# A graph layer on one core: 71 instead of 24 rows per step fetched one by one

## The chip, the cores and the metric

The kernel runs on one core of a Trainium2 chip. The metric is the device time of one execution in microseconds (us). A core has five engines with queues of their own: TensorE (PE; its weight loads are listed as PEld), VectorE (DVE), ScalarE (ACT), GpSimd (POOL) and SyncE (SP). SP and ACT can issue DMAs whose descriptors hardware makes; POOL's indirect DMA gathers rows by a list of numbers.

## The reference

The kernel computes one layer of message passing over a graph with 50000 nodes of 128 features and 1650000 edges, sorted by their target node:

```python
Xs = X[src]
m_data = Xs @ W_data.T + b_data
m_ctrl = Xs @ W_control.T + b_control
msg = jnp.where((edge_types == 0)[:, None], m_data, m_ctrl)
agg = jax.ops.segment_sum(msg, dst, num_segments=X.shape[0])
x = _layernorm(x + relu(agg + (X @ W_self.T + b_self)), axis=-1)
```

Each edge takes the row of its source node, multiplies it with one of two matrices, by the edge's type, and adds the result to its target node. Then come the node's own product, a relu, the residual and a normalisation of each row. Source nodes are random; the targets come in ascending order.

## The kernel before

Sums and matrices change places: the kernel first adds up the source rows of each target and type, and multiplies the sums with the two matrices afterwards. It goes over the edges in blocks (`NBLK` of them, all unrolled into one program). A block has two steps (`Q`), and a step three kinds of edges:

- 12 chunks (`R`) of 128 edges. `gathers` (L477) has POOL fetch 128 source rows of 512 bytes with one indirect DMA (L483), 24 of them a block. Six make a pass (`PASS`), with one buffer `y` a pass out of ten (`SLOTS`); the first gather of a pass waits until PE has read its buffer. In `products` (L494) PE multiplies the rows with a one-hot matrix of the targets (`oh`, which DVE makes in `onehot`, L411), and adds up into `acc` (L502).
- 43 fill edges (`F`) that `fill` (L308) puts in place of edges from a node to itself, which need no gather.
- `S` single rows, 24 of them in the kernel before. `single_rows` (L443) fetches each with a DMA of its own of 512 bytes, 12 of a step's on SP and 12 on ACT (`TURNS`). They land in one tile `yx` of `S` partitions, of which there are four (`ROW_SLOTS`), and are one more matmul a step (L508).

The byte offset of each single row is worked out by DVE (`offsets`, L432, tile `at_x`), loaded into registers by the queue that issues (a register load, L452), and moved into the DMA's address (a MOVE and the DMA, both L457). `LOADS` tells in how many portions the rows of a block are loaded and issued. A portion is at most 32 registers a queue:

```python
return min(n, 32 * part)
```

The rows of block b are asked for two blocks ahead (`AHEAD`). PE waits for all of them at once, when the first step of the block ends (`rows_fetched`, L462, a wait at L466 on one counter for each queue). PE takes its work in order, so that everything behind this wait waits too: the two products of single rows, the second step, `layer` (L533) of this block, and the sums that DVE takes from `acc` (`add`, L514).

The loop from L628 on writes the order of every engine's instructions out by hand. For block b, with its four passes numbered q:

- q = 0: six gathers and their products; `layer` and `moments` of block b-1; the one-hot matrix of b+2; portion 0 of the single rows of b+2.
- q = 1: six more, and the row product; ACT's `root` (L563) for the two blocks before, every second block; `counts` of b+2 (L422); portion 1, if there is one.
- q = 2: `columns` of the next group of ten blocks (`GB`), once a group; DVE's `store` (L572), which waits for the root; `left_out_rows`, and `fill` of b+5; portion 2, if there is one.
- q = 3: `left_out_matrix` of b+5; `offsets` of b+3 (L437); SP's `store_rows` (L577), which waits for `store`.

SP also loads a tile `xT` a block (L408), three blocks ahead, and once a group the lists of the next group (L167, L170, L172, L300, L305). Register loads of block places are at L401 (SP) and at L515 and L525 (DVE).

Of the kernel before, what the change touches and what calls it, by code (L numbers as in the profile page):

```python
# [38 lines left out]
B = 112  # L39
C = R * Q  # L40
F = 43
TURNS = (12, 12)
S = sum(TURNS)
LOADS = 1
BEGIN = (0, -(-Q * TURNS[0] // 4) * 4)
X = BEGIN[1] + -(-Q * TURNS[1] // 4) * 4
R1 = R + 1
# [36 lines left out]
def plain(b):  # L84

    return b == 0 or b >= NBLK - 1
# [6 lines left out]
def straight(ctx, tc, c, x, x_t, edges_t, edges_f, src_x, dst_first, first_p, out):  # L93
# [324 lines left out]
    def counts(b):  # L418

        cnt = ohp.tile([P, Q, 2 * W], BF16, name="cnt")  # L420
        with nc.allow_low_precision(reason="whole numbers up to R1"):
            nc.vector.tensor_reduce(cnt, ohs[b].rearrange("p (q r) w -> p q w r", r=R1), AX.X, ALU.add)  # L422
        cnts[b] = cnt
# [8 lines left out]
    def offsets(b):  # L432

        if not plain(b):
            g, i = divmod(b, GB)
            ats[b] = stp.tile([1, X], I32, name="at_x", bufs=AHEAD + 2)
            nc.vector.tensor_scalar(ats[b], one_g[g][:, i * X:(i + 1) * X], float(ROW), None, op0=ALU.mult)  # L437

    def part_of(n, part):

        return min(n, 32 * part)

    def single_rows(b, part):  # L443

        if part == 0:
            ys[b] = stp.tile([S, Q, D], F32, name="yx", bufs=ROW_SLOTS)
        both = []
        for j, (eng, dma) in enumerate(((SP, nc.sync), (ACT, nc.scalar))):
            n = Q * TURNS[j]
            k0, k1 = part_of(n, part), part_of(n, part + 1)  # L450
            at = BEGIN[j]
            _, rows = nc.values_load_multi_w_load_instructions(ats[b][0:1, at + k0:at + k1], engines=[eng], **RANGE)  # L452
            both.append([(dma, fetched[j][b % ROW_SLOTS], *divmod(k0 + k, TURNS[j]), sum(TURNS[:j]), row)
                         for k, row in enumerate(rows)])
        for pair in zip_longest(*both):
            for dma, sem, q, k, at, row in filter(None, pair):
                copy = dma.dma_start(ys[b][at + k:at + k + 1, q, :].bitcast(U8), x_bytes[:, bass.ds(row, ROW)])  # L457
                copy.then_inc(sem, 16)
                tc.no_tile_sem_insts.add(copy.ins.name)
                tc.add_to_no_dep_group(f"single{b}", copy.ins)  # L460

    def rows_fetched(b):  # L462

        times = len(range(b % ROW_SLOTS or ROW_SLOTS, b + 1, ROW_SLOTS))
        for j in range(2):
            wait = nc.tensor.wait_ge(fetched[j][b % ROW_SLOTS], 16 * Q * TURNS[j] * times)  # L466
        tc.declare_fence(wait.ins, group=f"single{b}")
# [149 lines left out]
    for b in range(1, RAHEAD):  # L617
# [3 lines left out]
        if b < AHEAD:  # L621
            onehot(b)
            counts(b)
            for part in range(LOADS):
                single_rows(b, part)
        if b == 1:
            clear_sums()
    for b in range(NBLK + 1):  # L628
# [16 lines left out]
        for q, (step, ks) in enumerate(passes_of(b)):  # L645
# [26 lines left out]
            if q == 3:  # L672
                left_out_matrix(b + RAHEAD)
                offsets(b + AHEAD + 1)
            if q < LOADS and not plain(b + AHEAD):
                single_rows(b + AHEAD, q)
# [336 lines left out]
```

## Time and profile before

| | |
|---|---|
| median of 3 runs | 18214.56 us (18202.21 to 18215.72) |
| the profiled execution | 18215.72 us, span 18214.0 us |
| blocks, gathers | 515; 12336 + 18 |
| single rows on SP and on ACT | 12312 each |
| busy: POOL, DVE, PE | 11699.9, 11018.7, 7203.9 us |
| DVE's costliest line (L422, `counts`) | 2973.1 us, 5773 ns each |
| the root on ACT (L563) | 258 times 295 ns |
| mean granted TensorE clock | 0.589 |

The profile's page gives the busy time of each engine, DMA queues (q0 has POOL's gathers, q1 what SP issues, q10 what ACT issues), and groups of instructions by line. A group's row has its count, its total and its mean duration, then the idle time of the engine before its instructions and what ended it: "issue" is time in which the profile shows no wait, "remote" an event that it can't put down to an engine. Instructions that issue DMAs on SP and ACT, moves and register loads are not counted as busy; they are seen in the timeline and in the answers for single lines.

### The profile page before, as it was taken

What the parts mean: (1) busy time and instruction counts of PE and PEld (TensorE: products, weight loads), DVE (VectorE), ACT (ScalarE), POOL (GpSimd) and SP (SyncE); (2) the same over time, 40 slices, a digit from 0 to 9 for tenths busy, and PEclk for the clock granted to TensorE, in tenths of its full rate; (3) what the DMA queues carried; (4) which work ended last, traced back from release to release, by engine and by line L of the source; (5) the groups of instructions that cost most, each with busy time, mean ns of one, the idle gap of its engine ahead of it and who ended that gap; (6) DMA issues with size and microseconds to landing.
All of it is one profiled execution on the core that took longest, in us unless ns stands there. A gap on an engine that the chain in (4) does not pass through costs nothing.

```text
span 18214.0 us, 162871 instructions
## 1 busy us (share of the span) xinstructions
PE 7203.9 (40%) x36190; PEld 6305.2 (35%) x36191; DVE 11018.7 (60%) x13887; ACT 79.5 (0%) x264; POOL 11699.9 (64%) x12364
## 2 busy tenths in 40 slices
PE   3343333433433333444333334443444334333344
PEld 3333333333333333333333333333333333333333
DVE  6666666566656656666666666666566666656555
ACT  0000000000000000000000000000000000000000
POOL 6666666666666666666666666666666666666665
PEclk6555555556555566555565555556555555656655
DMA  2222212222222221222222222222222222222221
GB/s 54 50 52 52 52 51 51 52 51 52 52 52 51 51 52 51 52 51 52 52 51 52 52 51 52 51 52 51 52 52 51 52 51 52 52 52 52 51 51 47
DMA packets 604666, 938.00 MB, mean 51 GB/s; under 512 B 308795, under 2 KB 392578, under 8 KB 603676
## 3 DMA queue, kind: packets, MB, share of 16 engines
q0 software_dynamic: 395392, 810.40, 17.6%
q1 hardware_dynamic: 183222, 110.53, 2.3%
q10 hardware_dynamic: 25062, 6.55, 0.2%
q8 instruction: 295, 4.83, 0.1%
q14 instruction: 695, 5.69, 0.1%
HBM read 896.80 MB, written 29.71 MB: 51 GB/s over the span
## 4 chain that ended last, share of the span: by engine, by line
DVE 44%; another core or an unknown queue 26%; PE 16%; issue 12%; ACTq 1%; DVEq 1%; DMA 0%; ACT 0%
DVE cnt L422 14%; PE acc L502 10%; DVE by L337 5%; DVE new L321 4%; DVE m L318 4%; DVE v_new L325 4%; DVE old L334 3%; PE po L541 2%; PE po L539 1%; ACTq L457 1%; DVE pl L369 1%; PE acc L508 1%; PE po L538 1%; DVE sums L518 1%
## 5 line engine op out<-in xcount | busy, mean ns | idle before, releaser
L483 POOL DMA_INDIRECT y<-in_x,idx x12336 | 11681.0, 947 | 6471.0 <-issue 3401.7
L502 PE MATMUL acc<-oh,y 128*128 128x120 f32 x24708 | 5141.9, 376 | 1832.3 <-issue 1828.4
L502 PEld LDWEIGHTS acc<-oh,y 128*128 128x128 f32 x24708 | 4697.9, 283 | 1955.6 <-issue 1952.4
L344 PE MATMUL small<-ones_b,by 128*86 128x1 bf16 x513 | 118.6, 231 | 7600.8 <-DVE by L337 5791.1
L422 DVE TENSOR_REDUCE cnt<-oh 128x240 bf16<-128x3120 f32 x515 | 2973.1, 5773 | 0.1
L344 PEld LDWEIGHTS <-by 128*86 128x86 bf16 x513 | 75.0, 146 | 7806.7 <-DVE by L337 5949.2
L547 DVE COPY h<-po 112x128 f32<-112x128 f32 x515 | 150.3, 292 | 4041.0 <-remote 2349.9
L414 DVE TENSOR_TENSOR oh<-col,small 128x3120 f32<-128x3120 f32 x515 | 1736.2, 3371 | 0.0
L518 DVE TENSOR_TENSOR sums<-acc,sums 128x180 f32 x1030 | 355.5, 345 | 2007.5 <-remote 1512.5
L337 DVE TENSOR_REDUCE by<-old 128x86 bf16<-128x1118 f32 x513 | 1110.8, 2165 | 19.1 <-DVE old L334 1.4
L508 PE MATMUL acc<-oh,yx 24*128 24x120 f32 x2052 | 648.3, 396 | 209.7 <-issue 209.2
L318 DVE TENSOR_TENSOR m<-rk,small 128x1118 f32<-128x1118 f32 x513 | 677.2, 1320 | 20.6 <-DVE small L316 2.8
L321 DVE TENSOR_TENSOR new<-m,small 128x1118 f32<-128x1118 f32 x513 | 677.3, 1320 | 17.6
L325 DVE TENSOR_REDUCE v_new<-new 128x26 f32<-128x1118 f32 x513 | 676.1, 1318 | 17.6
L334 DVE TENSOR_TENSOR old<-m,small 128x1118 f32<-128x1118 f32 x513 | 673.3, 1312 | 0.0
L508 PEld LDWEIGHTS acc<-oh,yx 24*128 24x128 f32 x2052 | 414.2, 244 | 391.7 <-issue 350.6
L541 PE MATMUL po<-wmsgT,sums 128*112 128x128 f32 x2060 | 526.6, 400 | 0.0
L351 DVE COPY at<-small 86x1 f32<-86x1 f32 x513 | 79.1, 154 | 614.7 <-remote 330.9
L539 PE MATMUL po<-bias,sums 3*112 3x128 f32 x1030 | 353.0, 438 | 242.1 <-issue 120.2
L511 PE MATMUL acc<-cnt,to_row 128*128 128x60 bf16 x2060 | 289.0, 211 | 362.0 <-issue 361.6
L541 PEld LDWEIGHTS po<-wmsgT,sums 128*112 128x112 f32 x2060 | 382.1, 255 | 109.9 <-issue 89.9
L539 PEld LDWEIGHTS po<-bias,sums 3*112 3x112 f32 x1030 | 207.0, 255 | 371.0 <-issue 229.8
(118 smaller groups left out, 4109.8 us busy)
## 6 DMA issues: line engine op xcount, KB each, us to landing
y<-in_x,idx POOLq DMA_INDIRECT x12336
yx<-in_x ACTq DMA_DIRECT2D x12312, 0.5 KB
yx<-in_x SPq DMA_DIRECT2D x12312, 0.5 KB
xT<-in_x_t SPq DMA_DIRECT2D x515, 56.0 KB
out<-o SPq DMA_DIRECT2D x515, 56.0 KB
vf_all<-vd SPq DMA_DIRECT2D x52, 430.0 KB
sdt<-in_edges_t SPq DMA_DIRECT2D x52, 390.0 KB
one_g<-in_src_x SPq DMA_DIRECT2D x52, 1.9 KB
```

What stands on the lines that cost most here:

```text
L318: nc.vector.tensor_tensor(m, rk_g[g][:, i, :, None].to_broadcast([P, C1, F]), rank_no_ps[:, None, :].to_broadcast([P, C1, F]), op=ALU.is_e ...
L321: nc.vector.tensor_tensor(new.rearrange("p (q r) f -> p q r f", r=R1), m.rearrange("p (q r) f -> p q r f", r=R1), vf.rearrange("p (q f) -> ...
L325: nc.vector.tensor_reduce(v, new, AX.X, ALU.add)
L334: nc.vector.tensor_tensor(old, m, cb[:, :, None].to_broadcast([P, C1, F]), op=ALU.mult)
L337: nc.vector.tensor_reduce(by, old.rearrange("p (q r) f -> p q f r", r=R1), AX.X, ALU.add)
L414: nc.vector.tensor_tensor(oh, col_g[g][:, i, :, None].to_broadcast([P, C1, 2 * W]), num_ps[:, None, :].to_broadcast([P, C1, 2 * W]), op=AL ...
L422: nc.vector.tensor_reduce(cnt, ohs[b].rearrange("p (q r) w -> p q w r", r=R1), AX.X, ALU.add)
L483: copy = nc.gpsimd.indirect_dma_start(out=y[:r, k % PASS, :].bitcast(U8), out_offset=None, in_=x_rows, in_offset=bass.IndirectOffsetOnAxis ...
L502: nc.tensor.matmul(acc[:, :2, :].rearrange("p t w -> p (t w)"), y[:r, k % PASS, :], ohs[b][:r, column(k), :], start=k == of_step[0], stop= ...
L508: nc.tensor.matmul(acc[:, :2, :].rearrange("p t w -> p (t w)"), ys[b][:, q, :], ohs[b][:S, q * R1 + R, :], start=False, stop=True)
L539: nc.tensor.matmul(po, a[0:3, 2, :B], bias, start=False, stop=False)
L541: nc.tensor.matmul(po, a[:, t, :B], c["wmsgT"][:, t * D:(t + 1) * D], start=False, stop=t == 1)
```

## The change

```diff
-TURNS = (12, 12)
+TURNS = (35, 36)
 S = sum(TURNS)
-LOADS = 1
+LOADS = 3
```

A step now has 71 single rows, 35 on SP and 36 on ACT; a block has 70 and 72. They are loaded and issued in three portions: 32, 32 and 6 on SP, 32, 32 and 8 on ACT. All else follows from these constants: a block covers 3300 edges (3206 before), so there are 501 blocks (515 before); `yx` has 71 partitions and `at_x` 144 numbers (48 before); the second and third portion of a block's rows are issued behind its second and third pass, on ACT behind the root.

## The prediction

> **What bounds the kernel now.** I read the page first: which engine fills the span.
>
> ```profile
> span 18214.0 us, 162871 instructions
> ...
> PE 7203.9 (40%) x36190; PEld 6305.2 (35%) x36191; DVE 11018.7 (60%) x13887; ACT 79.5 (0%) x264; POOL 11699.9 (64%) x12364
> ...
> q0 software_dynamic: 395392, 810.40, 17.6%
> q1 hardware_dynamic: 183222, 110.53, 2.3%
> q10 hardware_dynamic: 25062, 6.55, 0.2%
> ...
> L483 POOL DMA_INDIRECT y<-in_x,idx x12336 | 11681.0, 947 | 6471.0 <-issue 3401.7
> ...
> L508 PE MATMUL acc<-oh,yx 24*128 24x120 f32 x2052 | 648.3, 396 | 209.7 <-issue 209.2
> ```
>
> POOL's gathers, busy time plus the idle before them, are 11681 + 6471 = 18152 us: the whole span. So I looked at POOL in order of time (start, duration, idle before):
>
> ```profile
> 9257.74 0.95 POOL L483 DMA_INDIRECT y<-in_x,idx  x1 [0.31 <-issue]
> 9258.99 0.95 POOL L483 DMA_INDIRECT y<-in_x,idx  x1 [0.30 <-issue]
> 9262.92 0.95 POOL L483 DMA_INDIRECT y<-in_x,idx  x1 [2.98 <-remote]
> 9264.17 0.95 POOL L483 DMA_INDIRECT y<-in_x,idx  x1 [0.30 <-issue]
> ```
>
> A gather follows the last after 1.25 us, and about every twelfth after 3.8 us. Counted over the trace: 11304 intervals of 1.252 us and 1049 long ones, mean 3.83. A block has 24 gathers and mostly two long intervals: 24 x 1.252 + 2 x 2.58 = 35.2 us, and 513 such blocks are 18.06 ms. The buffer that a long interval waits for had been read by PE a median 10 us before, so this is mostly POOL's own pace, not PE's. DVE is busy 11018.7 / 515 = 21.4 us of a block and comes second.
>
> Then the two queues that the change loads, SP and ACT. In SP's timeline (start, length, what):
>
> ```profile
> 9171.70 21.93 SPq L457 DMA_DIRECT2D yx<-in_x  x24
> 9193.71 0.67 SPq L408 DMA_DIRECT2D xT<-in_x_t  x1
> 9204.60 20.41 SPq L457 DMA_DIRECT2D yx<-in_x  x24
> 9229.67 2.10 SPq L577 DMA_DIRECT2D out<-o  x2
> 9232.82 0.70 SPq L408 DMA_DIRECT2D xT<-in_x_t  x1
> 9241.50 22.82 SPq L457 DMA_DIRECT2D yx<-in_x  x24
> ```
>
> 24 single rows occupy SP for 20 to 23 of 35 us, although the median register move and the median issue of one are short (ns: least, median, most):
>
> ```profile
> L457 SPq MOVE yx<-in_x x12312: 2/29/1467, 33.1 to 18157.1; - x199
> L457 SPq DMA_DIRECT2D yx<-in_x x12312: 2/228/1487, 34.5 to 18157.8; - x199
> ```
>
> So I split one burst: first ten microseconds with gathers running, then three in which POOL paused.
>
> ```profile
> 9251.17 8.52 SPq L457 DMA_DIRECT2D yx<-in_x  x6
> ```
>
> ```profile
> 9261.77 2.55 SPq L457 DMA_DIRECT2D yx<-in_x  x7
> ```
>
> ```profile
> 9251.00:9261.00 10.00, 0.38 (x2) 0.10 (x1) 8.25 (x7) 0.00 (x0) 6.80 (x8) 0.63 0.20 53
> 9261.20:9264.20 3.00, 0.00 (x0) 0.00 (x0) 2.86 (x6) 0.00 (x0) 0.98 (x2) 0.50 0.00 1
> ```
>
> The last two lines are windows; the last two numbers of each are the DMA share and GB/s. With gather packets moving (0.20, 53 GB/s) a row takes SP 1.4 us; with none (0.00, 1 GB/s) 0.36 us. Over the whole trace I called a moment "traffic" when a q0 packet was in flight or had ended within 1.3 us: 88.6% of the time. In bursts SP spends 1.19 us a row in traffic and 0.43 out of it; ACT 0.84 and 0.353. SP alone, with ACT and PE idle, still needs 1.26 in traffic: the cause is not the other queue's rows. What the mechanism is I can't say.
>
> **The change, part by part.**
>
> *Fewer blocks.* A step takes 1536 + 43 + 71 = 1650 edges instead of 1603, a block 3300 instead of 3206. 1650000 - 3072 = 1646928 edges give 499 full middle blocks (513 before) and a rest of 228 in 2 gathers (2250 in 18 before). Gathers: 24 + 499 x 24 + 2 = 12002 instead of 12354. At 18177.5 / 12354 = 1.471 us each, the 352 that go are worth -518 us if POOL stays the bound: 17.70 ms. DVE and PE lose 14 blocks as well.
>
> *More rows on SP and ACT.* SP issues 2 x 35 = 70 a block instead of 24, ACT 72. This decides. SP's other work in a block: three register loads instead of one. The rows for them:
>
> ```profile
> L452 SPq TENSOR_LOAD <-at_x x513: 8/1583/1603, 31.7 to 18126.8; - x171
> ```
>
> ```profile
> L515 DVEq TENSOR_LOAD <-place_i x1030: 298/304/548, 90.9 to 18203.1; - x172
> ```
>
> 24 registers 1.583 us, one 0.304: (1.583 - 0.304) / 23 = 0.056 a register. Loads of 32, 32 and 6 are 2.04 + 2.04 + 0.58 = 4.7 us (before 1.6). With 1.2 us of stores (2.1 to 2.6 per two blocks), about 0.5 for xT and 1.1 for moves, waits on semaphores and a tenth of a group's lists, 7.5 us.
>
> Traffic lasts 0.886 x 35.37 = 31.3 us a block, set by 24 gathers and as long afterwards. If SP's 7.5 us fall outside it, SP issues 31.3 / 1.19 = 26.3 rows in traffic and the other 43.7 in 18.8 us: 31.3 + 18.8 + 7.5 = 57.6 us. If they all fall inside, 23.8 / 1.19 = 20 rows and then 50 x 0.43 = 21.5: 52.8 us. I take the middle, 55.2, against 35.2 of POOL. ACT: 31.3 / 0.84 = 37.3 rows, 34.7 x 0.353 = 12.2, loads 5.0: 48.5, under SP. The price from both sides: 70 x 0.43 + 7.5 = 37.6 us if all rows went at the quiet rate, 70 x 1.19 + 7.5 = 90.8 if none did. I stay between because POOL must pause once it is ten passes ahead of PE, and PE waits at L466 for the rows: the pauses are where SP catches up.
>
> Two pages of the Trainium skill say something else here. "DMA: Bandwidth & Descriptors", section "Issuing engines are not separate DMA queues", has the sequencer's time to start a DMA as usually small relative to the DMA; here ACT's q10 moved 25062 packets in 0.2% of 16 engines' span, some 23 ns each, beside 840 ns of issue, so the trace says the reverse for these rows, and by the rule the sum would be 17.70 ms. "Runtime: NRT & Kernel Launch", section "Instruction fetch mechanics", gives about 200 ns a register for such loads; an estimate from it is 14 us a block and some 32 ms, and the row of 1.583 us for 24 decides against it.
>
> *Who waits.* PE stops at L466 in mid-block; behind it stand the last row products, two passes, and DVE's sums. On ACT the root of a pair now stands behind 32 rows instead of 24 and ahead of 40; DVE's stores, `fill` and `offsets` stand behind it. With PE waiting for rows DVE has 55 - 21 us to spare, so I cost it at nothing; if that cover were gone it is up to (2.1 + 32 x 0.84) / 2 = 14.5 us a block. SP's stores come 46 rows later, with `o` in 4 buffers, and xT is asked for three blocks ahead: nothing. POOL's order is the same.
>
> *Small parts.* L508 contracts 71 rows instead of 24: the rows with 3 (438 ns, L539) and 128 partitions (400 ns, L541) differ little, 0. `at_x` grows from 1x48 (185 ns) to 1x144; 1x520 takes 412 ns (L201), so at most 0.1 us a block on a DVE that waits, 0 here. A group's row list is 5.6 KB instead of 1.9, one DMA in ten blocks: 0.
>
> *Sum.* 499 x 55.2 = 27545 us; ahead of SP's first row are 34 us and behind its last 56: **27.6 ms**, made against a span of 18214.0 us (execution 18215.7, median of the runs 18214.6).
>
> **Rivals.**
> 1. *The queues keep up, POOL stays the bound: 17.70 ms, faster.* It needs a block of SP under 36.2 us (18214 less 90, over 501), so a row in (36.2 - 7.5) / 70 = 0.41 us on average. For it: the medians (29 and 228 ns) and the quiet stretch (0.36). Against: 88.6% of the time is traffic.
> 2. *The queues almost keep up:* the slow spells fade once POOL waits, all rows go at 0.43: 37.6 us, 18.9 ms. Against: traffic can't be less than 24 gathers of 1.25 us a block.
> 3. *SP goes at ACT's rates* (0.84, 0.353): 46.0 to 50.3 us, 23.0 to 25.2 ms. For it: nothing in the rows tells why SP is the slower.
> 4. *Traffic spreads over the longer block*, so today's mean of 0.91 us in the bursts holds (21.9 / 24): 70 x 0.91 + 7.5 = 71.2 us, 35.6 ms. For it: PE frees buffers a pass at a time.
>
> **How the numbers follow.** Forecast 0.65 (23 to 33 ms with its own doubts), rival 1 0.07, 2 0.04, 3 0.12, 4 0.12. The range takes in rival 3 and reaches towards 4: 23.0 to 34.0 ms. About 0.2% is what a measurement tells from no change; cases 2, 3, 4 and the forecast are slower, rival 1 faster, and 0.01 lies between: 0.07, 0.01, 0.92.
>
> **What would show it.** Right: the rows' issues fill SP from end to end, 70 in 45 to 50 us; POOL's idle time doubles or more and its releaser is PE; PE's idle moves to L508 or the fence before it; block period near 55 us. Wrong: SP idle at 0.4 us a row (rival 1 or 2); ACT full and SP waiting; or DVE's `rstd` waiting for `sd` at length, which would make ACT's order, not SP's rate, the cause.

## The result and the profile after

The changed kernel takes 25257.88 us (median of 4 runs, 25222.15 to 25267.41) against 18208.39 us: 1.3871 times as long, 95% interval 1.3847 to 1.3895. It is slower, as forecast, and inside the range (23.0 to 34.0 ms), 8.5% under the 27.6 ms named.

For what follows one thing must be known: the experiments ran on four chips of two kinds. On chips 1 and 2 the kernel before takes 18.24 and 18.05 ms, as above; on chips 3 and 4 it takes 15.47 ms. Every ratio below is to the kernel before on the same chip. I call them 18 ms chips and 15 ms chips; the measurement above belongs with the first. Each chip was used in one session, so that the kind may be a chip's own or a condition it was in.

The page of the changed kernel (first run, profiled; span 25253.8 us): the lines that answer to those of before, and the shares of the chain that ended last.

```profile
span 25253.8 us, 254178 instructions
...
PE 6887.4 (27%) x35177; PEld 6389.4 (25%) x35178; DVE 10793.1 (43%) x13519; ACT 77.3 (0%) x257; POOL 11344.9 (45%) x12012
...
SPq 60%; issue 35%; DMA 2%; PE 1%; DVE 1%; ACTq 0%; another core or an unknown queue 0%; PEldq 0%; ACT 0%; DVEq 0%
SPq L457 51%; SPq L452 8%; DMA yx<-in_x 1%; DMA out<-o 1%; SPq L408 1%; PE acc L508 1%; SPq L401 0%; DVE cnt L422 0%; PE acc L502 0%; SPq L577 0%; ACTq L457 0%; DVE by L337 0%; PE pl L363 0%; DVE sums L518 0%
...
L483 POOL DMA_INDIRECT y<-in_x,idx x12000 | 11341.5, 945 | 13814.1 <-PE acc L502 9126.1
...
L508 PE MATMUL acc<-oh,yx 71*128 71x120 f32 x1996 | 595.2, 392 | 12940.7 <-PEq L466 12755.7
```

POOL, DVE, ACT and PE's products are busy for less time than before (PE's weight loads 1% longer), and the span is 7 ms longer. The chain now runs through SP: L457 (row moves and issues) 51%, L452 (row loads) 8%, and 35% "issue", time in which the queue waited for nothing that is shown. POOL's idle time has doubled, 13.8 ms against 6.5, and is ended mostly by PE's reading of buffers (L502, 9.1 ms). PE in turn stands 12.8 ms in front of L508, released by the fence of L466.

SP's timeline of two blocks (start, length, what):

```profile
12004.63 47.44 SPq L457 DMA_DIRECT2D yx<-in_x  x70
12052.16 0.36 SPq L408 DMA_DIRECT2D xT<-in_x_t  x1
12054.78 45.40 SPq L457 DMA_DIRECT2D yx<-in_x  x70
12100.35 2.03 SPq L577 DMA_DIRECT2D out<-o  x2
```

70 rows fill 45 to 47 us, loads included, and SP goes from one block's rows to the next block's without a wait. POOL in the same stretch:

```profile
12035.20 0.94 POOL L483 DMA_INDIRECT y<-in_x,idx  x1 [0.30 <-issue]
12036.45 0.94 POOL L483 DMA_INDIRECT y<-in_x,idx  x1 [0.30 <-issue]
12057.59 0.94 POOL L483 DMA_INDIRECT y<-in_x,idx  x1 [20.20 <-PE acc L502]
```

POOL gathers for some 31 us and then stands for 20. The windows just before and inside this stand (the last two numbers are the DMA share and GB/s), and SP's rows in each:

```profile
12020.00:12036.00 16.00, 5.64 (x24) 4.86 (x23) 4.35 (x5) 0.00 (x0) 10.24 (x11) 0.50 0.19 47
12039.50:12057.00 17.50, 3.64 (x19) 3.53 (x20) 2.73 (x2) 0.00 (x0) 0.00 (x0) 0.50 0.03 6
```

```profile
12018.84 17.57 SPq L457 DMA_DIRECT2D yx<-in_x  x18
```

```profile
12039.21 12.86 SPq L457 DMA_DIRECT2D yx<-in_x  x35
```

18 rows in 17.6 us with gathers running, 35 in 12.9 us without, with one register load among them each time. That is the loss in one view: POOL must stand still before SP can catch up.

### The profile page after: what moved, and what is told of

Same layout as the page of the kernel before. It is cut to its first block, busy times and chain, and to the rows that moved or that the text cites. A ratio compares the mean times of both kernels' runs of the same rounds, so it can differ in the third digit from the quotient of the medians.

```text
span 25253.8 us, 254178 instructions
## 1 busy us (share of the span) xinstructions
PE 6887.4 (27%) x35177; PEld 6389.4 (25%) x35178; DVE 10793.1 (43%) x13519; ACT 77.3 (0%) x257; POOL 11344.9 (45%) x12012
## 4 chain that ended last, share of the span: by engine, by line
SPq 60%; issue 35%; DMA 2%; PE 1%; DVE 1%; ACTq 0%; another core or an unknown queue 0%; PEldq 0%; ACT 0%; DVEq 0%
SPq L457 51%; SPq L452 8%; DMA yx<-in_x 1%; DMA out<-o 1%; SPq L408 1%; PE acc L508 1%; SPq L401 0%; DVE cnt L422 0%; PE acc L502 0%; SPq L577 0%; ACTq L457 0%; DVE by L337 0%; PE pl L363 0%; DVE sums L518 0%
## 5 line engine op out<-in xcount | busy, mean ns | idle before, releaser
L483 POOL DMA_INDIRECT y<-in_x,idx x12000 | 11341.5, 945 | 13814.1 <-PE acc L502 9126.1
L502 PE MATMUL acc<-oh,y 128*128 128x120 f32 x24004 | 5037.4, 396 | 9.3 <-issue 9.2
L502 PEld LDWEIGHTS acc<-oh,y 128*128 128x128 f32 x24004 | 4800.3, 305 | 10.5 <-issue 10.3
L508 PE MATMUL acc<-oh,yx 71*128 71x120 f32 x1996 | 595.2, 392 | 12940.7 <-PEq L466 12755.7
L508 PEld LDWEIGHTS acc<-oh,yx 71*128 71x128 f32 x1996 | 421.3, 263 | 13061.4 <-PEq L466 12872.7
L538 PE MATMUL po<-wselfT,xT 128*112 128x128 f32 x1002 | 310.0, 412 | 0.0
L531 DVE TENSOR_TENSOR sums<-pl,sums 128x336 f32<-128x336 f32 x499 | 253.4, 508 | 79.1 <-issue 63.0
L511 PEld LDWEIGHTS <-to_row 128*128 128x128 bf16 x2002 | 264.4, 132 | 32.6 <-issue 4.5
```

Of the source, the lines that this page charges most:

```text
L483: copy = nc.gpsimd.indirect_dma_start(out=y[:r, k % PASS, :].bitcast(U8), out_offset=None, in_=x_rows, in_offset=bass.IndirectOffsetOnAxis ...
L502: nc.tensor.matmul(acc[:, :2, :].rearrange("p t w -> p (t w)"), y[:r, k % PASS, :], ohs[b][:r, column(k), :], start=k == of_step[0], stop= ...
L508: nc.tensor.matmul(acc[:, :2, :].rearrange("p t w -> p (t w)"), ys[b][:, q, :], ohs[b][:S, q * R1 + R, :], start=False, stop=True)
```

## The experiments

| kernel (single rows a step on SP, ACT) | chip | us | against before there |
|---|---|---|---|
| changed (35, 36) | as above, 18 ms | 25258 | 1.387 [1.385, 1.390] |
| changed, again | 1, 18 ms | 25337 | 1.389 [1.387, 1.391] |
| changed, again | 2, 18 ms | 24923 | 1.381 (one run) |
| changed, one gather a pass | 1, 18 ms | 15460 | 0.848 (one run) |
| changed, one gather a pass | 3, 15 ms | 15413 | 0.996 (one run) |
| changed, three gathers a pass | 3, 15 ms | 15581 | 1.007 (one run) |
| changed, fixed addresses | 1, 18 ms | 19055 | 1.045 (one run) |
| (35, 1) | 2, 18 ms | 22196 | 1.230 (one run) |
| (35, 1) | 3, 15 ms | 15660 | 1.012 (one run) |
| (1, 36) | 3, 15 ms | 15343 | 0.992 (one run) |
| (16, 16) | 2, 18 ms | 18199 | 1.008 [1.007, 1.010] |
| (1, 1) | 1, 18 ms | 18070 | 0.991 (one run) |
| (6, 6) | 4, 15 ms | 15581 | 1.007 [1.006, 1.009] |

### Gathers taken away, and rows on one queue: the first four

One gather a pass (three: 3 in place of each 1 below):

```diff
-        for k in ks:
+        for k in ks[:1]:
...
-        seen[i] += 16 * len(ks)
+        seen[i] += 16 * len(ks[:1])
...
-            nc.tensor.matmul(..., y[:r, k % PASS, :], ...)
+            nc.tensor.matmul(..., y[:r, k % PASS % 1, :], ...)
```

Rows on one queue (the fourth kernel has (1, 36)), with the portions skipped that a queue has no rows for:

```diff
-TURNS = (35, 36)
+TURNS = (35, 1)
...
+            if k0 == k1:
+                both.append([])
+                continue
```

> The changed kernel with one gather a pass instead of six: POOL fetches the first chunk's rows and the pass's six products all read these, so five sixths of the gathered sums are left out; single rows, register loads and every instruction of PE, DVE, SP and ACT stay. Theory T (a row costs SP about 1.03 us while gather packets move and 0.35 us otherwise, and SP's issue sets the block): 4 gathers leave some 8 us of traffic a block, 8 / 1.03 = 8 rows there, 62 x 0.35 = 22 us for the others, 6 us for loads and stores: 34 to 37 us a block, 17.0 to 18.5 ms. Rival O (70 rows in a row are slow whatever else runs, by the queue's own rows or their landing): 50 us a block as in the changed kernel, 25.2 ms.

> The changed kernel with three gathers a pass instead of six; the other three products of a pass read the same rows, so half of the gathered sums are left out. Theory T: 12 gathers, 16 us of traffic a block, 16 / 1.03 = 15.5 rows there, 54.5 x 0.35 = 19 us, 6 us for loads and stores: 41 us, 20.7 ms (19.8 to 21.8). Rival O: 25.2 ms. A third reading, that POOL's gathers themselves are the bound in the changed kernel, would halve the block: 13 ms or what DVE allows.

> 35 single rows of a step on SP and 1 on ACT (a step has 36; 511 blocks). SP issues 70 rows a block as in the changed kernel, ACT 2 instead of 72. Theory T: SP sets the block alone, 50.4 us x 511 = 25.8 ms (25.0 to 26.2). Rival S (both queues draw on one shared capacity, so that the sum of their rows counts): 72 rows a block instead of 142, 35 to 38 us, 18.1 to 19.4 ms.

> 1 single row of a step on SP and 36 on ACT (a step has 37; 511 blocks). ACT issues 72 rows a block, SP 2. Theory T with ACT's own rates in the changed kernel (0.83 us in traffic, 0.33 outside): 31.4 us of traffic hold 36 rows, the other 36 take 12 us, loads 3 to 5 us: 44 to 48 us, 22.5 to 24.5 ms. If ACT's rate in traffic was better only because it had pauses, it comes out like SP alone, near 50 us, 25.8 ms. Rival S: 18.1 to 19.4 ms.

Measured on chip 3: 15413, 15581, 15660 and 15343 us, and 15468 for the kernel before. None of the theories had a case for this: there was no loss here to explain. The row issues of (35, 1), all gathers present (ns: least, median, most; this kernel has three lines more, so that L457 is L460 here and L577 is L580):

```profile
L460 SPq MOVE yx<-in_x x35630: 29/29/29, 28.2 to 15632.5; - x200
L460 SPq DMA_DIRECT2D yx<-in_x x35630: 227/228/538, 28.3 to 15632.5; - x200
```

No move takes longer than 29 ns, where before's reached 1467. SP's timeline in that run:

```profile
9020.61 26.25 SPq L460 DMA_DIRECT2D yx<-in_x  x70
9047.03 2.08 SPq L580 DMA_DIRECT2D out<-o  x2
9050.14 0.38 SPq L408 DMA_DIRECT2D xT<-in_x_t  x1
9053.21 26.36 SPq L460 DMA_DIRECT2D yx<-in_x  x70
```

70 rows in 26.3 us with two loads among them, gathers or not, and a block of SP in 30.6 us (15660 / 511). POOL, counted in the trace of (1, 36), issues 12251 of 12254 times after 1.250 us on average: its long intervals are gone too. So both slownesses that the prediction started from, SP's in traffic and POOL's every twelfth gather, come and go together with the kind of chip. Two things follow for such a chip. POOL bounds the kernel before, 12354 x 1.25 = 15.44 ms (measured 15.47), without pauses. And with 70 rows SP takes 31.1 us a block (15581 / 501 in the run with three gathers a pass, where POOL has slack), just over POOL's 30.0. The changed kernel itself was not run on a 15 ms chip; from these two numbers I estimate 15.6 ms, some 0.7% over before.

### The changed kernel on chip 1, and three cuts

> The changed kernel itself, against the kernel before on the same chip. In the four runs just made the kernel before took 15468 us, not 18208, rows cost SP 0.34 us whether gather packets moved or not, and POOL had no long intervals. Theory C (the slow issue of rows and POOL's long intervals belong to a chip or its condition, and the loss of 39% needs them): where before is near 15.5 ms, SP needs 70 x 0.34 + 5.2 for loads + 2 = 31 us a block against 30 of POOL: 501 x 31 = 15.5 ms, within 1% of before. Where before is near 18.2 ms, 25.2 ms again. Rival K (the loss belongs to the changed kernel, and the four runs were quick only because each left out part of the load): about 39% over before in either case.

Chip 1 is an 18 ms one (before 18235.68 us): 25336.86 us, ratio 1.389. The loss is repeatable there. So theory C's second half holds; its first half, that a 15 ms chip loses almost nothing, was not put to a direct test.

The changed kernel with one gather a pass, same edit as above:

> The changed kernel with one gather a pass instead of six, five sixths of the gathered sums left out, as in the run before. Where the kernel before takes near 18.2 ms: theory T (gather packets make rows slow there) 17.0 to 18.5 ms, since 8 of 70 rows fall in traffic; rival O (rows are slow there whatever else runs) 25.2 ms. Where before is near 15.5 ms: 15.4 ms as before, set by SP's 31 us a block.

Measured: 15460.24 us, against 25337 for the same instructions of SP and ACT with all gathers. Rival O falls. SP's timeline:

```profile
9023.03 26.41 SPq L457 DMA_DIRECT2D yx<-in_x  x70
9049.62 2.89 SPq L577 DMA_DIRECT2D out<-o  x2
9052.61 0.38 SPq L408 DMA_DIRECT2D xT<-in_x_t  x1
9055.22 20.00 SPq L457 DMA_DIRECT2D yx<-in_x  x54
```

The rows run as on the other kind of chip, 26.4 us for 70. Theory T was short, though: it kept 1.03 us for rows in what traffic is left and so expected 17.0 to 18.5 ms. Counted as in the prediction, rows in traffic cost 0.338 us here and outside 0.340. Four gathers a block, apart from one another, slow nothing. The cut takes away POOL's work, its packets and the records of both at once; which of them matters it can't tell.

One row a step on each queue, against the kernel before:

```diff
-TURNS = (12, 12)
+TURNS = (1, 1)
```

> One single row of a step on SP and one on ACT, one portion; a step has 2 rows, 522 blocks, 12525 gathers; nothing else changes. It tells whether POOL's long intervals need the single rows. Where before is near 18.2 ms: if POOL's long intervals are its own, 1.471 us a gather, 18.4 ms; if the rows' issue on SP and ACT makes them, 1.25 us a gather, 15.7 to 16.0 ms. Where before is near 15.5 ms: 12525 x 1.25 = 15.66 ms, 1.2% over before by the gathers alone.

Measured: 18070.38 us, 0.991. POOL's timeline:

```profile
9037.01 0.94 POOL L483 DMA_INDIRECT y<-in_x,idx  x1 [0.30 <-issue]
9042.65 0.94 POOL L483 DMA_INDIRECT y<-in_x,idx  x1 [4.69 <-PEq L490]
9043.89 0.94 POOL L483 DMA_INDIRECT y<-in_x,idx  x1 [0.30 <-issue]
```

With 4 rows a block left the long intervals are still there: 680 of them, mean 4.75 us, mostly 18 or 24 gathers apart instead of 12. A gather takes 1.440 us on average instead of 1.471. So the rows don't make POOL's pauses; they add a little to them. And with so few rows SP is slow all the same (start, length; SP's and ACT's two rows of one block):

```profile
9032.68 3.28 SPq L457 DMA_DIRECT2D yx<-in_x  x2
9032.79 0.79 ACTq L457 DMA_DIRECT2D yx<-in_x  x2
```

Over the run the second of two rows costs SP 2.0 us in traffic, and ACT 0.32.

The row's address fixed, in the changed kernel, so that no register is needed:

```diff
-x_bytes[:, bass.ds(row, ROW)]
+x_bytes[:, (b * 97 + at + k) % N * ROW:][:, :ROW]
```

> The changed kernel with each single row fetched from a fixed address instead of one from a register, so that the register move before each row is gone and the row loads stay (the sums take other rows than the reference's). Where before is near 18.2 ms: if every instruction of a queue is slowed in traffic (0.5 us each), a row costs half, 57 rows fit in the 30 us of traffic, 40 us a block, 20 ms; if the DMA alone is slowed and the move stands behind it, 46 us, 23 ms. Where before is near 15.5 ms: a row is 0.26 us, SP needs 70 x 0.26 + 7 = 25 us, POOL is the bound again: 12002 x 1.25 = 15.0 ms.

Measured: 19054.54 us, 38.0 us a block. The expectation was wrong in one point: with nobody to use the registers, the row loads went as well (4.2 us a block on SP). The rows' cost is as the first reading had it. In traffic a row costs SP 0.594 us instead of 1.095, ACT 0.478 instead of 0.880: the move is gone, and the cost is about halved. The traces show the two instructions apart. Counted in traffic with the gap ahead of each, the changed kernel's move takes SP 0.50 us and its DMA 0.56 on this chip; with fixed addresses the DMA takes 0.56 too. In (35, 1) on chip 3 they are 0.07 and 0.26. The move itself takes 0.25 us instead of 0.03, and it only sets an address. So each instruction is slowed, and a slow transfer alone would not do that. The time of 19.05 ms says less: SP no longer sets every block, and PE waits at L466 for 3.5 ms instead of 12.8.

### One queue's rows on an 18 ms chip, and a smaller step

> The changed kernel again, beside the kernel before on the same chip, to see which kind of chip this is and what the change does there. Theory C: where before takes near 15.5 ms, rows cost SP 0.34 us throughout and a block is SP's 31 us: 15.5 to 15.7 ms, 0 to 1.5% over before. Where before takes near 18.2 ms: 25.3 ms. Rival K (39% over before on every chip): 21.5 ms where before takes 15.5.

> 35 single rows of a step on SP and 1 on ACT (a step has 36; 511 blocks): SP's load as in the changed kernel, ACT's nearly gone. Where before takes near 18.2 ms: theory T, each queue is slowed by itself and SP sets the block, 50.5 x 511 = 25.8 ms (25.0 to 26.2); rival S, both queues draw on one shared capacity: 72 rows a block instead of 142, 35 to 38 us, 18.1 to 19.4 ms. Where before takes near 15.5 ms: 15.7 ms as before.

Chip 2 is again an 18 ms one (before 18051.13 us). The changed kernel takes 24922.90 us there. (35, 1) takes 22195.95: 43.4 us a block, between the two theories.

```profile
9036.81 40.40 SPq L460 DMA_DIRECT2D yx<-in_x  x70
9077.31 0.36 SPq L408 DMA_DIRECT2D xT<-in_x_t  x1
9079.89 20.34 SPq L460 DMA_DIRECT2D yx<-in_x  x34
```

SP still sets the block, but its rows go faster with ACT's gone: 0.608 us in traffic against 0.971 in the changed kernel on the same chip (0.357 and 0.352 outside). So the two queues do take from each other while gathers run. Put as instructions, with a move and a DMA for each row, SP and ACT together issue in traffic:

| | SP | ACT | instructions per us |
|---|---|---|---|
| changed, chip 1 | 1.095 us a row | 0.880 | 2 / 1.095 + 2 / 0.880 = 4.1 |
| fixed addresses, chip 1 | 0.594 | 0.478 | 1 / 0.594 + 1 / 0.478 = 3.8 |
| changed, chip 2 | 0.971 | 0.777 | 2 / 0.971 + 2 / 0.777 = 4.6 |
| (35, 1), chip 2 | 0.608 | almost none | 2 / 0.608 = 3.3 |

In these long bursts the sum stays between 3.3 and 4.6 instructions a microsecond, with moves or without. Outside traffic SP alone reaches 2 / 0.35 = 5.7, and ACT as much beside it. One limit that both queues share does not come out of this, though. At 4.1 to 4.6 SP alone would need 0.43 to 0.49 us a row in (35, 1), and it took 0.61. In (1, 1) SP needs 2.0 us for a row with ACT all but idle, and ACT 0.32. And in the trace of the kernel before, the second to fifth row of a burst cost ACT 0.32 us each in traffic, where SP's cost 1.0 to 1.7. So SP is slow without ACT's rows too; in long bursts ACT's rows add to it. What sets the rate, these runs don't show.

16 rows on each queue, against the kernel before:

```diff
-TURNS = (12, 12)
+TURNS = (16, 16)
```

> 16 single rows of a step on each queue, one portion (a step has 32; 513 blocks, 12292 gathers). Where before takes near 18.2 ms, SP would fit 25 rows into 30 us of traffic at 1.15 us and 7 more into the pauses: 35 to 36 us a block, as POOL's 35.2: between -0.5% (62 gathers fewer) and +2%. Rival: if rows cost anything before a queue is full, say through POOL's long intervals, more than +2%. Where before takes near 15.5 ms: POOL stays the bound, -0.5%.

Measured on the 18 ms chip: ratio 1.0084, 95% interval 1.0067 to 1.0101. It lies in the expected range, on the losing side: 62 gathers fewer are worth 0.5%, and POOL takes 18184 / 12292 = 1.479 us a gather against 18051 / 12354 = 1.461 on that chip. SP isn't full (24.4 + 3.3 us of rows and 1.9 of loads in 35.4), so 8 rows more on each queue already crowd POOL.

(1, 1) was quicker than the kernel before, so the step between could be quicker still:

```diff
-TURNS = (12, 12)
+TURNS = (6, 6)
```

> 6 single rows of a step on each queue, one portion (a step has 12; 519 blocks, 12447 gathers instead of 12354). With 24 rows a step POOL took 1.471 us a gather where before takes 18.2 ms, with 2 rows 1.440 (18070 us against 18236, 0.9% less, one run). If the rows crowd POOL a little even where the queues keep up, the middle is 1.455 us x 12447 = 18.1 ms, 0.3 to 1.2% under before. If they don't, and the gathers count alone, 0.7% over. Where before takes near 15.5 ms, POOL issues at 1.25 us whatever the rows: 0.7% over.

The chip was a 15 ms one: ratio 1.0073, interval 1.0059 to 1.0086, which is what 93 gathers more cost at 1.25 us. There the gathers count alone. Whether (6, 6) wins on an 18 ms chip stays open.

## Why the prediction was right, and where not

- *POOL bounds the kernel before, at its own pace:* right. Its pace differs by chip, 1.25 us a gather or 1.46 to 1.48 with pauses, and with hardly any single rows the pauses stay.
- *SP's issue of 70 rows sets the block:* right; the page's chain, POOL's releaser and PE's wait behind L466 are as named. With five gathers in six gone the block falls to 30.9 us.
- *Traffic of 31.3 us a block, as long afterwards:* 0.623 x 50.4 = 31.4.
- *The sum, 55.2 us a block:* measured 25253.8 / 501 = 50.4. The terms that were mis-sized are the rates of a row. In traffic 29.4 rows went in 30.3 us, 1.03 us each where 1.19 was taken from bursts of 24. Outside, 39.8 rows took 13.9 us, 0.349 each instead of 0.43. SP's other work was 4.4 us of loads (4.7) and 1.8 us (2.8) of everything else. Why a row costs less in the longer bursts isn't shown.
- *"The cause is not the other queue's rows":* right only in part. I read it off moments in which SP was alone and had 1.26 us a row. Taking ACT's rows away for the whole run brings SP from 0.97 to 0.61, so they add to its cost; but 0.61 is far over the 0.36 outside traffic, and in (1, 1) SP's row takes 2.0 with ACT all but idle.
- *ACT under SP:* right. On chip 2 rows and loads take ACT 20.4 + 14.5 + 5.0 = 39.9 us a block and SP 29.2 + 13.1 + 4.3 = 46.6.
- *The root behind 32 rows costs nothing:* right. DVE's reciprocal waited for it 68.7 us in the whole run.
- *Small parts:* right. L508 takes 392 ns with 71 rows, 396 with 24.
- *The Trainium skill:* "Runtime: NRT & Kernel Launch", section "Instruction fetch mechanics", has about 200 ns a register for register loads; ACT's loads of 32 registers took 2141 ns (median of all its loads), 67 each. "DMA: Bandwidth & Descriptors", section "Issuing engines are not separate DMA queues", has starting a DMA as usually small beside the DMA; here issuing the rows set the block.
- *Rival 3, SP at ACT's rates,* gave 46.0 to 50.3 us, and the measured 50.4 lies just over it, nearer to it than to my 55.2. The time alone can't tell the two apart; the trace can. Outside traffic SP did go at 0.349, about ACT's 0.353, but in traffic at 1.03, between 0.84 and 1.19. *Rival 4* needed 0.91 us over all rows, and they took (30.3 + 13.9) / 69.2 = 0.64.
- *Rival 1, the queues keep up,* needed a row under 0.41 us. On a 15 ms chip it costs 0.34, so there the rival's condition holds, and the gain would be lost to SP's loads and stores instead (31.1 us against 30.0). I gave it 7 in 100 and read one chip's slowness as the kernel's. No run shows whether the one trace could have told the two apart. The forecast was made from the trace of an 18 ms chip and is borne out on 18 ms chips alone; that its result came from one as well was luck.

## What to carry to other kernels

Before a queue is given more small DMAs, find what one costs in each company it keeps: split its bursts by what else runs, and multiply. The median (29 and 228 ns here) hides the spells that set the sum. And where a trace shows stalls of several queues at once with no wait behind them, run the kernel before on a second chip: the size of a loss like this one can depend on it (39% measured on the one kind, 0.7% estimated for the other).

## What the runs showed of the hardware

On two of four chips, and in the measurement above, the issue of instructions on SP and ACT is slow while POOL's gathers run at 1.25 us each: 3.3 to 4.6 a microsecond in sum over bursts of 70 rows. It goes in steps: of the moves over 300 ns in the trace of before, half take 693 to 709 ns. POOL itself pauses 2.6 us there, mostly every 6 to 18 gathers. The kernels traced on the other two chips show neither. The traces differ in one more thing: counted in them, the kernel before on an 18 ms chip left 71029 semaphore updates with 162871 instructions, (35, 1) on a 15 ms chip 311519 with 187104, and (35, 1) on an 18 ms chip 109571 with the same instructions. Where issue is slow, records of semaphores are missing. With one gather a pass few are missing on chip 1 (205437 updates, and 216398 for the same instructions on chip 3), and there the rows are fast. And where issue is slow some moves are recorded with 1 or 2 ns, while (35, 1) on chip 3 has none under 29. That would fit a profiler whose records can't be written fast enough and hold the engines up, and it would fit other causes; no run here tells them apart. Every run here has its span from such records, so whether the 18 ms are the program's own time is open.
